# Forming gelu's argument inside a PSUM bank, and taking the order of all instructions from a table

## The chip, the cores and the metric

The kernel runs on one core of a Trainium2 chip. The metric is the device time of one execution, in microseconds (us). Before the change it is 719.35 us, the median of three runs (719.32 to 719.5).

The five engines are called here as the profile calls them: PE (TensorE, matrix products), ACT (ScalarE), DVE (VectorE), POOL (GpSimd), SP (SyncE, which issues most DMAs). Each engine works through its own list of instructions in the order in which the program put them there, and instructions of different engines are held apart by semaphores. PSUM, where PE writes its sums, is made of eight banks; one tile of 128x512 fp32 values fills one of them.

## The reference

A feed-forward layer on x of 4 sequences by 1024 tokens by 512 features, with a gate, and a residual:

```
scale = cond @ norm_w.T + 1.0
h = x * (scale * rsqrt(mean(x * x) + EPS))
val, gate = split(h @ up_w.T)               # 2 x 2048 columns
h = val * gelu(gate)
hq = act_quant(h)                           # 8-bit steps, by the largest |h| of a token
wq = weight_quant(down_w)                   # ternary
y = hq @ wq.T + x
```

## The kernel before, in words

**Tiling.** The four sequences are four batches of 1024 tokens. Each batch is cut in two halves of 512 tokens (TOK), and the 2048 gated columns in 16 groups of 128. One such group is a *slot*; 55 of the slots go through `slot()` (the first ones of the first batch go through simpler functions). A slot computes value and gate for both token halves, a 2x2 block product, by a scheme of seven products in place of eight. `product(c, g, ...)` is one of the seven (0 to 6): six matmuls of 128x512, since weights and activations are split in two fp16 parts, of which three cross terms over two halves of 256 features are kept.

**The slot's sums.** Three kinds of PSUM banks are used: two A, one B, two E. The products of slot g are laid into them so that sums which several results share are formed once:

- product 0 into bank A; ACT copies A to bank B; product 1 accumulates on B; ACT's gelu reads B into `t1` (the gate of the first half);
- product 4 into bank E; ACT copies E into `v` in SBUF;
- product 5 accumulates on A, which then holds 0+5. ACT copies this to `t2` in SBUF (L1217 to L1219, `first_value`);
- product 6 accumulates on A after that; DVE adds A into `v` (L1255);
- one slot later product 3 accumulates on A (0+5+6+3), and DVE multiplies it with `t1` into the result (L1239); product 2 accumulates on E (4+2), DVE adds E and `t2` into `t2` (L1249), ACT's gelu turns `t2` in place (L1252), and DVE multiplies it with `v` (L1258).

**The down projection.** The ternary weights of the down projection are fp8, and a second 2x2 scheme (class `Pair`, 11 pairs of token blocks) runs while the next batches' slots run, four pairs at a time in slots 10 to 13 of a batch, and three pairs at the end. A product of a pair is eight matmuls of 128x256 (L1413), which fill half of a PSUM bank. The pair's steps are spread over the slot: `first` forms product B11 in half 1 of bank k1, has ACT copy it to half 0 (L1421), and adds product B21 there; `third` accumulates product T2 on half 1 of k1 and has ACT copy that half to half 1 of bank k2 (L1430, 128x256); `fourth` goes on with B22 onto half 1 of k1, T3 on k2. Thus B21 and the copy touch different halves of the same bank k1. The last tokens go through a plain down projection (L1362).

**The order.** No function emits an instruction at once. The engines that the code calls are recorders: each call is kept as a step, and at the end a planner decides in which order the steps go out. In the kernel before this is class `Plan`: it works out which step needs which (by the regions that each reads and writes), gives each step a price, a due time and a place on its engine, runs some rounds of mending with chosen random seeds (`MENDS`), moves single steps by a list (`MOVES`), and `emit` then calls the real engines in the order of planned start times. The order within an engine, and where among PE's matmuls an ACT step is emitted, both come from there. The semaphores between engines are put in when the steps are emitted, from the order in which they are emitted.

**Start.** PE first runs warm-up matmuls (L1510), turns the first token tiles (L1494, L825) and then begins with the first slots (L1198, L1199); ACT loads its table for gelu in a step of its own (`start_t`, L1461) before it squares and scales x (L1480, L1487) and evicts the turned x (L1498).

## Time and profile before

| | |
|---|---|
| median of 3 runs | 719.35 us (719.32 to 719.5) |
| the profiled execution, its span | 717.4 us (the chain's last piece ends at 717.44) |
| what lies around the span (median less span) | 1.9 us |
| PE busy | 711.5 us (99%), 3625 matmul records |
| DVE busy | 605.2 us (84%) |
| ACT busy | 409.8 us (57%) |
| POOL busy | 130.0 us (18%) |
| granted TensorE clock | 1.000 |
| ACT copy `t<-A` (L1219) | 55 of 585 ns, 32.2 us |
| DVE add `t<-E,t` (L1249) | 55 of 689 ns, 37.9 us |

How to read it: the span is the time from the first to the last instruction that the profiler saw, and the time of a run is a little longer. A group of instructions is named by line, engine and operation, then out<-in with the shape. Idle time of an engine counts only where that engine, or one that waits for it, is on the path to the end. The busy time of PE includes matmuls that are in flight; one 128x512 matmul takes 379 ns from start to end, but the next starts long before.

### The profile page before, as it was taken

What the parts mean: (1) busy time and instruction counts of PE and PEld (TensorE: products, weight loads), DVE (VectorE), ACT (ScalarE), POOL (GpSimd) and SP (SyncE); (2) the same over time, 40 slices, a digit from 0 to 9 for tenths busy, and PEclk for the clock granted to TensorE, in tenths of its full rate; (3) what the DMA queues carried; (4) which work ended last, traced back from release to release, by engine and by line L of the source; (5) the groups of instructions that cost most, each with busy time, mean ns of one, the idle gap of its engine ahead of it and who ended that gap; (6) DMA issues with size and microseconds to landing.
All of it is one profiled execution on the core that took longest, in us unless ns stands there. A gap on an engine that the chain in (4) does not pass through costs nothing.

```text
span 717.4 us, 10113 instructions
## 1 busy us (share of the span) xinstructions
PE 711.5 (99%) x3625; PEld 355.8 (50%) x3625; DVE 605.2 (84%) x903; ACT 409.8 (57%) x671; POOL 130.0 (18%) x138
## 2 busy tenths in 40 slices
PE   8999999999999999999999999999999999999998
PEld 4544444444444456664444445665444444445744
DVE  7978998899899899878899887767878888956897
ACT  5677688784546897553435786533333775332454
POOL 4753141020100004660023003700011000000000
PEclk9999999999999999999999999999999999999999
DMA  7778999999785896759234555778233444453414
GB/s 261 253 205 208 240 227 252 194 257 268 219 227 133 210 245 173 223 153 211 67 101 110 118 129 142 176 191 173 73 118 103 102 102 99 99 98 104 150 57 146
DMA packets 189134, 118.74 MB, mean 166 GB/s; under 512 B 151302, under 2 KB 158359, under 8 KB 189084
## 3 DMA queue, kind: packets, MB, share of 16 engines
q1 hardware_dynamic: 188794, 117.77, 64.3%
q8 instruction: 28, 0.46, 0.3%
q10 hardware_dynamic: 290, 0.33, 0.1%
q14 instruction: 22, 0.18, 0.1%
HBM read 59.20 MB, written 23.09 MB: 115 GB/s over the span
## 4 chain that ended last, share of the span: by engine, by line
PE 97%; DMA 1%; ACT 1%; POOL 0%; DVE 0%; issue 0%; SPq 0%; POOLq 0%
PE A L1141 40%; PE E L1141 20%; PE B L1141 10%; PE po L1413 9%; PE E L1156 6%; PE A L1156 4%; PE B L1156 3%; PE po L1362 2%; PE E L1362 1%; PE A L1362 1%; DMA H<-in_x_dram 1%; PE B L1413 1%; PE B L1362 0%; PE A L1199 0%; PE po L1494 0%; PE po L825 0%
## 5 line engine op out<-in xcount | busy, mean ns | idle before, releaser
L1141 PEld LDWEIGHTS <-SXY 128*128 128x128 f16 x2184 | 213.7, 98 | 250.9
L1141 PE MATMUL A<-R,SXY 128*128 128x512 f16 x1188 | 276.3, 379 | 0.0
L1141 PE MATMUL E<-R,SXY 128*128 128x512 f16 x594 | 145.3, 379 | 0.0
L1334 DVE TENSOR_TENSOR H<-H,am 128x1024 f32<-128x1024 f32 x64 | 76.6, 1222 | 0.2
L1141 PE MATMUL B<-R,SXY 128*128 128x512 f16 x312 | 76.6, 379 | 0.0
L1275 DVE TENSOR_REDUCE gm<-H 128x512 f32<-128x1024 f32 x56 | 69.0, 1232 | 0.9
L1252 ACT ACTIVATE t<-t,sg 128x512 f32<-128x512 f32 x55 | 39.7, 721 | 51.0 <-DVE t L1249 51.0
L1239 DVE SCALAR_TENSOR_TENSOR H<-A,sg,t 128x512 f32<-128x512 f32 x55 | 41.2, 749 | 31.9 <-PE A L1141 31.6
L1291 POOL PARTITION_ALL_REDUCE am<-R x8 | 15.5, 1934 | 288.4 <-DVE R L1277 288.4
L1236 ACT ACTIVATE t<-B,sg 128x512 f32<-128x512 f32 x55 | 37.8, 687 | 42.7 <-PE B L1141 42.6
L1227 ACT COPY B<-A 128x512 f32<-128x512 f32 x55 | 31.4, 571 | 53.3 <-PE A L1141 53.1
L1249 DVE TENSOR_TENSOR t<-E,t 128x512 f32<-128x512 f32 x55 | 37.9, 689 | 28.2 <-PE E L1141 27.7
L1413 PE MATMUL po<-wd,R 128*128 128x256 fp8e4 (+1 forms) x448 | 57.0, 275 | 0.0
L1219 ACT COPY t<-A 128x512 f32<-128x512 f32 x55 | 32.2, 585 | 43.4 <-PE A L1141 39.0
L1255 DVE TENSOR_TENSOR v<-A,v 128x512 f32<-128x512 f32 x55 | 37.9, 690 | 20.4 <-PE A L1141 19.6
L1413 PEld LDWEIGHTS <-R 128*128 128x128 bf16 (+1 forms) x480 | 47.0, 98 | 13.1
L1231 ACT COPY v<-E 128x512 f32<-128x512 f32 x55 | 32.2, 586 | 31.9 <-PE E L1141 15.6
L1342 ACT ACTIVATE H<-H 128x1024 f32<-128x1024 f32 x38 | 39.7, 1049 | 8.5 <-DVE H L1334 8.3
L1258 DVE SCALAR_TENSOR_TENSOR H<-v,sg,t 128x512 f32<-128x512 f32 x55 | 41.7, 759 | 1.7 <-ACT t L1252 1.4
L1156 PEld LDWEIGHTS <-SXY 128*128 128x128 f16 x264 | 25.8, 98 | 30.5
L1346 ACT ACTIVATE R<-H 128x1024 bf16<-128x1024 f32 x38 | 39.6, 1052 | 1.0 <-DVE H L1086 0.5
L1277 DVE TENSOR_TENSOR R<-R,gm 128x512 f32<-128x512 f32 x56 | 38.4, 686 | 0.9
(270 smaller groups left out, 919.2 us busy)
## 6 DMA issues: line engine op xcount, KB each, us to landing
SXY<-s_dram SPq DMA_DIRECT2D x57, 256.0 KB, 2.7
H<-in_L_cond_up_w_dram SPq DMA_DIRECT2D x13, 512.0 KB, 4.1
SXY<-s_dram SPq DMA_DIRECT2D x15, 384.0 KB, 3.7
xr<-in_x_dram SPq DMA_DIRECT2D x19, 256.0 KB, 2.9
out_dram<-xr SPq DMA_DIRECT2D x19, 256.0 KB, 2.1
s_dram<-SXY SPq DMA_DIRECT2D x12, 384.0 KB, 3.6
s_dram<-SXY SPq DMA_DIRECT2D x5, 896.0 KB, 6.7
H<-in_x_dram SPq DMA_DIRECT2D x8, 512.0 KB, 4.8
```

Of the source, the lines that this page charges most:

```text
L1141: PE.matmul(o, s[:, w, k, :], xs(l, k), start=start and n == 0, stop=stop and n == len(TERMS) - 1, skip_group_check=True,)
L1156: PE.matmul(ps, a[k // 2][:, w, k % 2, :], XP[:, l, k, h * TOK : (h + 1) * TOK], start=n == 0, stop=n == len(terms) - 1,)
L1239: DVE.scalar_tensor_tensor(h_half(g - 1, 0), prev["A"], gain(g - 1, 0), prev["t1"], ALU.mult, ALU.mult)
L1249: DVE.tensor_tensor(prev["t2"], prev["E"], prev["t2"], ALU.add)
L1252: ACT.activation(prev["t2"], prev["t2"], AF.Gelu, scale=gain(g - 1, 1))
L1258: DVE.scalar_tensor_tensor(h_half(g - 1, 1), prev["v"], gain(g - 1, 0), prev["t2"], ALU.mult, ALU.mult)
L1275: DVE.tensor_reduce(gm[0], v, AX.X, ALU.max, apply_absolute_value=True)
L1277: return [largest, lambda: DVE.tensor_tensor(m, m, gm[0], ALU.max)]
L1334: DVE.tensor_tensor(v, v, r.to_broadcast([P, 2, TOK]), ALU.mult)
L1342: ACT.activation(v, v, AF.Copy, bias=MAGIC)
L1346: ACT.activation(q, by_tile(v), AF.Copy, bias=-MAGIC)
L1413: PE.matmul(po, w[:, j], m, start=start and j == 0, stop=stop and j == n - 1, skip_group_check=True,)
```

## The change

Two things are changed together.

**In the slot.** After product 5, ACT no longer copies bank A to `t2`. DVE adds A (which holds 0+5) and `v` (the kept product 4) into bank E, product 2 accumulates on E one slot later, and gelu reads E from PSUM into `t2`. The DVE add that stood behind product 2 is gone. So there are 55 ACT copies less, and 55 DVE adds stand at another place with other operands.

**In the order.** The planner is taken out: its dependency search, prices, due times, mending and moves. The steps are still recorded, and the order in which they are emitted is read from a table, `ORDER`, which holds the difference from each step's number to the next, packed as text.

```diff
         def first_value():
             product(5, g, cur["A"], False, True)
-            cur["t2"] = wpool.tile([P, TOK], F32, name=f"t2_{g}", tag="t2")
-            ACT.copy(cur["t2"], cur["A"])
+            DVE.tensor_tensor(cur["E"], cur["A"], cur["v"], ALU.add)
...
         if prev:
             product(2, g - 1, prev["E"], False, True)
-            DVE.tensor_tensor(prev["t2"], prev["E"], prev["t2"], ALU.add)
         mid[1]()
         if prev:
-            ACT.activation(prev["t2"], prev["t2"], AF.Gelu, scale=gain(g - 1, 1))
+            prev["t2"] = wpool.tile([P, TOK], F32, name=f"t2_{g}", tag="t2")
+            ACT.activation(prev["t2"], prev["E"], AF.Gelu, scale=gain(g - 1, 1))
...
-class Plan:
+class Book:
...
     def order(self):
 
-        steps = self.steps
...
-        for n in MENDS:
-            order, kept = self.mend(order, kept, random.Random(n))
-        return self.moved(order)
...
+        packed = zlib.decompress(base64.b85decode("".join(ORDER)))
+        order, at = [], 0
+        for n in range(0, len(packed), 2):
+            at += int.from_bytes(packed[n : n + 2], "little", signed=True)
+            order.append(self.steps[at])
+            at += 1
+        assert len({s.n for s in order}) == len(self.steps)
+        return order
+
+    def emit(self):
+        lines = {}
+        for s in self.order():
+            if s.line not in lines:
+                lines[s.line] = _at_line(s.line)
+            lines[s.line](s.do, s.args, s.kwargs)
+
+
+ORDER = (
+    'c-m!J37k%K_doX;qZzZA8M82!VF-~eYbaErO{<g^ylro9ucF@SEot#qDne1&Dy2;-3Pq@FWr>CeO=dC-hOv#oFwZ^z?>XmppJ(cS',
...
-    book.tied = False
...
-    book.emit(book.order())
+    book.emit()
```

Over the whole program PE has 3621 matmuls and 3558 weight loads, DVE 898 instructions, POOL 148 and SP 367 before and after; ACT has 54 fewer (55 copies less, one table load more). The order is another on every engine. Lines move up by some 360: what was L1141 (a product's matmul in later batches) is L782, L1413 is L1050, L1421 is L1058, L1430 is L1067, L1439 is L1076, L1498 is L1133, L1510 is L1145. The new DVE add is L859, the gelu that reads E is L892.

The places that the prediction speaks of follow. The first is PE at the beginning of the last three pairs (the third place in the program where pairs begin). `po_99` is bank k1 of the first of them, `xn_111` holds the operand of product T2, `R` here that of product B21. Before:

```order
L1413 LDWEIGHTS xn_111
L1413 MATMUL po_99<-wd,xn_111 128x256
L1413 LDWEIGHTS R
L1413 MATMUL B_90<-wd,R 128x512
L1413 LDWEIGHTS R
L1413 MATMUL B_90<-wd,R 128x256
```

This is the last of T2's eight matmuls on k1, and behind it a product of the next pair in bank `B_90`. In the change:

```order
L1050 LDWEIGHTS xn_111
L1050 MATMUL po_99<-wd,xn_111 128x256
L1050 LDWEIGHTS R
L1050 MATMUL po_99<-wd,R 128x256
L1050 LDWEIGHTS R
L1050 MATMUL po_99<-wd,R 128x256
L1050 LDWEIGHTS R
L1050 MATMUL po_99<-wd,R 128x256 [waits Activation_49]
```

Behind T2's last matmul stand here the eight matmuls of B21 on the other half of the same bank; the third of them waits for ACT, and what it waits for is the copy of half 1 (now L1067), which in turn waits for the second matmul of B21.

There are ten such copies from `po_99` to `po_97`. In the kernel before, between the matmul that releases the copy and the first later matmul on its bank, PE has at each of them at least six matmuls of 128x512, or eight of 128x256 and four of 128x512, on other banks. In the change five of the ten stand inside the eight matmuls of B21: at three (the first pair of batch 1's slots, the first pair of batch 2's, and the first of the last three pairs) nothing stands between, at one (second pair of batch 1) one matmul of 128x512, at one (fourth pair of batch 1) one of 128x256. At the other five there are at least six of 128x512, or nothing on PE waits for the copy soon.

The second place is ACT's list around the copy that belongs to it. Before:

```order
L1252 ACTIVATE t_1_123<-t_1_123,sg_124 128x512 [waits DVE_49]
L1421 COPY po_99<-po_99 128x256 [waits PE_49]
L1430 COPY po_97<-po_99 128x256 [waits PE_49,Activation_49]
L1421 COPY B_90<-B_90 128x256 [waits PE_49]
L1439 COPY po_97<-po_97 128x256 [waits PE_49,Activation_49]
```

In the change:

```order
L1058 COPY po_99<-po_99 128x256 [waits PE_49]
L892 ACTIVATE t_1_123<-E_100,sg_124 128x512 [waits PE_49]
L876 ACTIVATE t_0_105<-B_90,sg_124 128x512 [waits Activation_49]
L1067 COPY po_97<-po_99 128x256 [waits PE_49,Activation_49]
L1058 COPY B_90<-B_90 128x256 [waits PE_49,Activation_49]
```

The copy from `po_99` to `po_97` is the step of `third`. Its place among ACT's copies is nearly the same, but two gelus now stand between it and the copy of `first`.

The third place is ACT's list at the start of the program. `ssq` is the sum of squares of x, `rs` the factor of the norm, `start_t` a tile that nothing reads. Before:

```order
L1461 ACT_TABLE_LOAD
L1461 ACTIVATE start_t_85<-one 128x1 [waits DVE_49]
L1480 ACTIVATE H,ssq_0_87<-H 128x512 [waits DMAHW2_49]
L1480 ACTIVATE R,ssq_0_87<-H 128x512
L1480 ACTIVATE R,ssq_0_87<-H 128x512 [waits DMAHW3_49]
L1487 ACTIVATE H<-H,rs_0_88 128x512 [waits Activation_49,Pool_49]
L1487 ACTIVATE H<-H,rs_0_88 128x512 [waits DVE_49]
L1498 ACTIVATE R<-po_98,scT 128x512 [waits DVE_49,PE_49]
```

In the change:

```order
L1115 ACT_TABLE_LOAD
L1115 ACTIVATE H,ssq_0_87<-H 128x512 [waits DMAHW2_49]
L1115 ACTIVATE R,ssq_0_87<-H 128x512
L1115 ACTIVATE R,ssq_0_87<-H 128x512 [waits DMAHW3_49]
L336 DMA R<-in_cond_dram 128x384 [waits DMAHW0_49]
L1122 ACTIVATE H<-H,rs_0_88 128x512 [waits DVE_49,Pool_49]
L1122 ACTIVATE H<-H,rs_0_88 128x512 [waits Activation_49]
L1097 ACT_TABLE_LOAD
L1097 ACTIVATE start_t_85<-one 128x1
L1133 ACTIVATE R<-po_98,scT 128x512 [waits DVE_49,PE_49]
```

The step `start_t`, which needs the table that holds gelu, has moved behind the scaling of x, and with it a second table load stands right ahead of the first eviction (L1133).

More of the change, by code (lines that the diff above doesn't have):

```diff
@@ L96, with __init__ @@
 class Step:
-    __slots__ = (
-        "n", "eng", "do", "args", "kwargs", "line", "cost", "alone", "port", "before", "wait", "deps", "after", "late", "soon", "start", "end", "tied", "own",
-        "margin", "guard", "behind", "queue", "pre", "due",
-    )
+    __slots__ = ("n", "eng", "method", "do", "args", "kwargs", "line")
 class Engine:
-    def __init__(self, plan, name, real):
-        self._plan, self._name, self._real = plan, name, real
+    def __init__(self, book, name, real):
+        self._book, self._name, self._real = book, name, real
     def __getattr__(self, method):
```

452 lines of the change are left out of this document (85 added, 367 removed), and 14 rows, old and new, of tables (MENDS, MOVES).

## The prediction

> **What bounds the kernel now.** I read the page's busy shares and chain first, then the waits of PE, then the chain around one of the places that the change rearranges.
>
> ```profile
> PE 711.5 (99%) x3625; PEld 355.8 (50%) x3625; DVE 605.2 (84%) x903; ACT 409.8 (57%) x671; POOL 130.0 (18%) x138
> PE 97%; DMA 1%; ACT 1%; POOL 0%; DVE 0%; issue 0%; SPq 0%; POOLq 0%
> ...
> PE A L1510 <- DVE H L607: 1.3, 1, 1.3
> PE po L1494 <- DVE H L1489: 0.5, 1, 0.5
> PE B L731 <- DVE dg L725: 0.5, 1, 0.5
> PE B L1199 <- ACT R L1498: 0.4, 1, 0.4
> ...
> 25.00:714.33 689.33, 689.32 (x3519) 344.44 (x3517) 585.20 (x833) 395.36 (x641) 115.48 (x116) 1.00 0.64 162
> ```
>
> PE is the bound, at full clock, and almost without a gap: the list of its waits is complete with four rows, all before 15 us, and in the stretch from 25 us to its last matmul it is busy 689.32 of 689.33 us. So 32 us less of ACT copies is worth nothing by itself: ACT (57%) and DVE (84%) have no share in the chain there. PE does the same matmuls after the change. The time can fall only by what PE idles at the start, and rises by each gap that the new order makes in PE's list. A gain of DVE or ACT counts only where it closes such a gap; there are none after 25 us.
>
> The size of PE's steps comes from the chain at a pair's beginning:
>
> ```profile
> 271.96 1.51 PE A L1141 x7
> 273.47 0.87 PE po L1413 x8
> 274.34 1.29 PE E L1141 x6
> 275.63 1.42 PE po L1413 x13
> ```
>
> Six matmuls of 128x512 take 1.29 us, 0.216 each; eight of 128x256 take 0.87, 0.109 each. Fp16 and fp8 products alternate here at no extra cost, so the finer mixing of the new table costs nothing by itself.
>
> **The change, part by part.** *The slot.* These groups hold the work removed, moved and replaced:
>
> ```profile
> L1219 ACT COPY t<-A 128x512 f32<-128x512 f32 x55 | 32.2, 585 | 43.4 <-PE A L1141 39.0
> L1249 DVE TENSOR_TENSOR t<-E,t 128x512 f32<-128x512 f32 x55 | 37.9, 689 | 28.2 <-PE E L1141 27.7
> L1252 ACT ACTIVATE t<-t,sg 128x512 f32<-128x512 f32 x55 | 39.7, 721 | 51.0 <-DVE t L1249 51.0
> L1236 ACT ACTIVATE t<-B,sg 128x512 f32<-128x512 f32 x55 | 37.8, 687 | 42.7 <-PE B L1141 42.6
> L1255 DVE TENSOR_TENSOR v<-A,v 128x512 f32<-128x512 f32 x55 | 37.9, 690 | 20.4 <-PE A L1141 19.6
> L1275 DVE TENSOR_REDUCE gm<-H 128x512 f32<-128x1024 f32 x56 | 69.0, 1232 | 0.9
> ```
>
> ACT loses 55 copies of 585 ns (32.2 us). DVE's add keeps its count; its new form, PSUM plus SBUF into PSUM, is in no row, so I bound it by the add that also reads A and `v` (690 ns) and by that plus what the PSUM side might cost more, as between gelu from SBUF and from PSUM (721 against 687 ns, here even less): 0.66 to 0.73, and I take 690. Gelu reads PSUM as L1236 does, 687 in place of 721. All of this lies beside PE. What touches PE is when banks come free. Bank A is released for product 6 by an add of 690 instead of a copy of 585, 0.1 us later, and on an engine that is busy 84% instead of 57%. Bank E is released by gelu (687) where the add (689) did it: nothing. Behind product 2 the chain add, gelu, multiply loses its first link, 0.69 us earlier for L1258. Product 2 comes a slot after the new add, so that wait is covered by many matmuls. Cost of the slot on the path: 0, as long as product 6 finds some 0.8 us of other PE work behind product 5 (four matmuls of 128x512); if DVE is inside a reduction of 1.23 us when A is ready, this cover is gone and PE waits up to that long.
>
> *The order at the pairs.* This is where PE gets new waits. At five of the ten copies L1430 (L1067 in the change) the copy and the next matmul on the same bank now stand with nothing, one 128x512 or one 128x256 between. PE finishes a matmul of B21, ACT copies half 1, and only then may PE go on with B21 on half 0. The rows for the price:
>
> ```profile
> L1413 PE MATMUL po<-wd,R 128*128 128x256 fp8e4 x438 | 55.8, 273 | 0.0
> L1430 ACT COPY po<-po 128x256 f32<-128x256 f32 x10 | 3.6, 360 | 6.1 <-PE po L1413 6.1
> ...
> 23.76 0.37 ACT L852 CAST R<-po 128x256 f16<-128x256 f32 x1 [1.49 <-PE po L825]
> 24.18 0.14 PEld L825 LDWEIGHTS po<-ident,H 128*128 128x128 f32 x1 [0.22 <-ACT R L852]
> ...
> 713.50 0.82 PE L1362 MATMUL po<-wd,R 128*128 128x256 fp8e4 x6
> 714.36 0.48 DVE L1371 SCALAR_TENSOR_TENSOR R<-po,dq,R 128x256 f32<-128x256 f32 x1 [0.17 <-PE po L1362]
> ```
>
> The matmul lasts 273 ns to its end. From PE's end to the reader's start it takes 0.04 (714.32 to 714.36). The copy lasts 0.36. From ACT's end to PE it takes 0.05 (24.13 to 24.18). Without a wait PE would start the next matmul 0.109 after the last. The gap is 0.273 + 0.04 + 0.36 + 0.05 - 0.109 = 0.61 us. With a 128x512 between it is 0.61 - 0.216 = 0.40, with a 128x256 0.61 - 0.109 = 0.50. Sum: 3 x 0.61 + 0.40 + 0.50 = 2.73 us. The rows of 23.76 and 24.18 show that such a loop does stop PE already now: a cast of half a bank, 0.37 us, and the weight load that waited for it came 0.22 late. In the kernel before the same pair of steps (L1413, L1430) never stops PE, because 1.29 us of product matmuls on bank E stand behind T2 (the chain at 274.34), and the copy at 0.36 ends far inside them. Its cover is what the new order takes away. ACT may still be in an instruction when the copy is released, and the copy stands in line: with ACT busy 57% and instructions of 0.7 us this is 0.57 x 0.35 = 0.2 us on average for each place, 1.0 in all; below, nothing. Since two gelus with early operands stand ahead of the copy in the row shown, I take 0 and keep 1.0 for the range. Behind the stalled matmul everything on PE is late by the same amount, DVE and ACT with it, so nothing downstream absorbs it.
>
> The wait is between two halves of one bank, so it could look needless. The Trainium skill's page "PSUM — Partial Sum Buffer", section "PSUM bank collisions raise a hardware error", has the rule that speaks against this order: guard PSUM by bank and quadrant, not by address, since two engines at different addresses of one bank still collide. The rows of 24.18 agree, as PE went on to the bank only after the cast had ended; by the rule none of the five waits can go and the sum stays, and if halves counted apart it would be nothing.
>
> *The start.* The rows:
>
> ```profile
> 1.28 1.28 ACT L1461 ACT_TABLE_LOAD   x1 [1.28 <-PEq L2092]
> 2.58 0.20 ACT L1461 ACTIVATE start_t<-one 128x1 f32<-128x1 f32 x1
> ...
> 13.04 1.84 ACT L1498 ACTIVATE R<-po,scT 128x512 f16<-128x512 f32 x3 [1.57 <-PE po L1494]
> ...
> 11.52 0.20 PEld L1494 LDWEIGHTS po<-ident,H 128*128 128x128 f32 x2 [0.32 <-ACT H L1487]
> 11.91 0.42 PEld L825 LDWEIGHTS E<-ident,H 128*128 128x128 f32 x4 [0.19 <-POOL H L817]
> 14.36 1.60 PEld L1199 LDWEIGHTS <-SXY 128*128 128x128 f16 x8 [0.55 <-issue]
> 16.51 0.11 PEld L1199 LDWEIGHTS <-SXY 128*128 128x128 f16 x2 [0.55 <-ACT SXY L852]
> ...
> 3.37 2.31 PE L1510 MATMUL A<-H 128*128 128x512 f16 x5
> 22.80 0.69 POOL L817 TENSOR_SCALAR H<-H,iv 128x512 f32<-128x512 f32 x1
> ```
>
> The gaps before weight loads between 11 and 25 us add up to 0.32 + 0.19 + 0.55 + 0.55 + 0.22 = 1.83 us; that is the most that any order can win there, as the loads' ordinary spacing is in it. The new order puts two warm-up matmuls (L1510, 2.31 / 5, some 0.4 each and partly overlapping, so 0.4) among the turns and a POOL scaling of weights (0.69) ahead of the second x tile: up to 1.1 us lost. I take 0 and keep -1.83 and +1.1. The second table load, 1.28, and `start_t`, 0.20, are 1.48 us and fit into the 1.57 us in which ACT waits for the turned x: 0.
>
> The Trainium skill's page "ScalarE: Activation LUTs", section "What ACT_TABLE_LOAD costs", has a switch at about 1283 ns of load and 1380 ns of drain. The load of 1.28 agrees; the drain is not seen, for `start_t` began at 2.58, right behind the load, but nothing was in ACT then. By the rule the sum would be 1.3 us more.
>
> *The sum.* The profiled execution goes from 717.4 to 717.4 + 2.73 = 720.2 us of span. It lies 1.9 us under the median of runs, which stays around it: 719.35 + 2.73 = **722.1 us**.
>
> **The rivals.** (A) *The new add gates product 6.* Mechanism: DVE in a reduction of 1232 when A holds 0+5, so A comes free at 0.04 + up to 1.23 + 0.69 + 0.05 = 2.0 us, 0.7 past the cover of a product (1.29). For it: DVE at 84%. Against: DVE's reads of A (L1255, L1239) are of this kind now, and no PE gap comes of it. Two or three such slots among 55 give 1.6 us: 723.7. (B) *The second table load does not fit.* If ACT must empty before a load, 1.3 us more on the way to L1498 and so to L1199, as the chain runs through both: 723.4. For it: only 0.09 us is to spare in the gap. Against: ACT has waited for PE for a microsecond by then, so there is nothing left to empty.
>
> (C) *Not slower.* The copy is released by T2's own last matmul, not by the last one on its bank, so that the B21 matmuls that stand behind T2 cover it. Then at the last pairs two matmuls lie between, 0.61 - 2 x 0.109 = 0.39, at the fourth pair of batch 1 three, 0.28, at the other three more than 0.6 us: 0.67 in all, 720.0, which is no change. It decides once PE's signal for T2 is what ACT waits on. For it: the code needs no more than T2. Against: B21's matmul in the rows shown waits for ACT although ACT reads another half, so waits go by bank, and a copy that comes after two of B21 must then wait for them. (D) *Faster.* (C), or ACT so early that it costs nothing, and the start's gaps closed: 719.35 - 1.83 = 717.5. For it: ACT has 32 us more room and a new order at the start. Against: five waits stand in the list. (E) *The waits as forecast, and the start's whole gain*: 719.35 + 2.73 - 1.83 = 720.3, again no change.
>
> **How the numbers follow.** A measurement of this kernel cannot tell less than 0.2% (1.4 us) from no change, so "same" is 717.9 to 720.8. The forecast (722.1, with its bounds 721.0 to 723.1) gets 0.52, A 0.14, B 0.11, C 0.11, D 0.07, E 0.05. Slower is the forecast, A and B: 0.77; same C and E: 0.16; faster D: 0.07. The range leaves out D and half of A's upper tail: it begins at 719.9, under C, and goes to 724.2, where the forecast with both 1.0 of ACT's queue and 1.1 of the start would stand.
>
> **What would show it.** In the changed profile the list of PE's waits has rows of a matmul L1050 on `po` behind ACT's L1067, five in number, near 273, 289, 320, 445 and 665 us, each 0.3 to 0.6 us of idle time (a little less than the gaps above, since the matmul in flight counts as busy). If they are absent, C is right and the step on the pairs is wrong. If PE's waits name DVE L859 with `A`, A is right; if the start has ACT's L1133 later than 13.04 behind two table loads, B is. PE busy in the middle should stay within 0.1 us of its stretch but for these five; the copies of 585 ns should be gone from ACT with no effect on the end. The prediction is wrong if PE's last matmul ends before 716 us of the span.

## The result, and the profile after

| | before | changed | ratio (95% interval) |
|---|---|---|---|
| median | 719.42 us (719.32 to 719.63, 4 executions) | 723.23 us (722.36 to 724.32, 4 executions) | 1.0051 (1.0038 to 1.0064) |
| span of the profiled execution | 717.4 us | 721.6 us | |

The change makes the kernel slower by 0.5%: 3.8 us by the medians, 4.2 us by the two profiled spans. The forecast was 722.1 us, the range 719.9 to 724.2. Two executions that lie far off all the others are left out below: 812.54 us with a granted clock of 0.878 (the copy done twice), and 1534.94 us (the kernel before).

The busy shares of the changed kernel:

```profile
PE 712.2 (99%) x3625; PEld 356.4 (49%) x3625; DVE 594.0 (82%) x903; ACT 372.1 (52%) x617; POOL 126.8 (18%) x138
```

PE has the same 3625 matmul records and 0.7 us more of busy time. ACT has 37.7 us less work than before and DVE 11.2 us less, and the kernel is slower: neither engine was the bound.

The waits of PE in the changed kernel (what waited for what; microseconds in total, times, the longest). It is the whole list:

```profile
PE B L341 <- DVE one L248: 3.3, 1, 3.3
PE po L1050 <- ACT po L1067: 2.1, 5, 0.5
PE B L782 <- ACT B L867: 0.5, 1, 0.5
PE A L1145 <- DVE neghalf L246: 0.4, 1, 0.4
```

The second row is the forecast one: five waits of B21's matmuls (L1050) for the copy of `third` (L1067). The third row was not forecast. The first and the last are at the start, ahead of 10 us.

The timeline of PE, and then of ACT, around the five places (start, length, engine and line, and in brackets the idle time ahead and its releaser). The first place is at 273 us, the others follow:

```profile
273.45 0.38 PE L1050 MATMUL po<-wd,R 128*128 128x256 fp8e4 x2
274.33 0.49 PE L1050 MATMUL po<-wd,R 128*128 128x256 fp8e4 x3 [0.50 <-ACT po L1067]
...
290.37 0.82 PE L1050 MATMUL po<-wd,R 128*128 128x256 fp8e4 x6 [0.27 <-ACT po L1067]
...
320.93 0.60 PE L1050 MATMUL po<-wd,R 128*128 128x256 fp8e4 x4 [0.38 <-ACT po L1067]
...
446.00 0.27 PE L1050 MATMUL po<-wd,R 128*128 128x256 fp8e4 x1 [0.50 <-ACT po L1067]
...
666.75 0.93 PE L1050 MATMUL po<-wd,R 128*128 128x256 fp8e4 x7 [0.50 <-ACT po L1067]
```

```profile
273.93 0.36 ACT L1067 COPY po<-po 128x256 f32<-128x256 f32 x1 [0.46 <-PE po L1050]
```

At the first place two matmuls of B21 are through at 273.45 + 0.38 = 273.83. ACT starts the copy of the other half of the bank 0.1 later, at 273.93, and ends at 274.29. PE goes on at 274.33. A matmul in flight counts as busy, so the delay is the idle time plus the length of the last matmul less the spacing at which the next would have come: 0.50 + 0.273 - 0.109 = 0.66 us at the three bare places, 0.27 + 0.379 - 0.216 = 0.43 where a matmul of 128x512 lies between, and 0.38 + 0.273 - 0.109 = 0.54 where one of 128x256 does. Together 2.95 us.

The wait that was not forecast is at 213 us. PE, then ACT:

```profile
211.25 1.46 PE L782 MATMUL E<-R,SXY 128*128 128x512 f16 x6
213.18 1.46 PE L782 MATMUL B<-R,SXY 128*128 128x512 f16 x6 [0.47 <-ACT B L867]
```

```profile
208.84 1.06 ACT L602 ACTIVATE xr<-nx 128x1024 bf16<-128x1024 f32 x1 [3.29 <-DMA nx<-in_L_cond_down_w_dram]
...
210.47 1.04 ACT L602 ACTIVATE xr<-xt 128x1024 bf16<-128x1024 f32 x1
...
211.51 1.04 ACT L602 ACTIVATE xr<-xn 128x1024 bf16<-128x1024 f32 x1
...
212.55 0.58 ACT L867 COPY B<-A 128x512 f32<-128x512 f32 x1
```

ACT's copy of bank A to bank B, which product 1 needs, stands in ACT's list behind three preparations of the ternary weights (L602). The first of these waited 3.29 us for its DMA, so all three run just when the copy is wanted. The delay of PE is 0.47 + 0.379 - 0.216 = 0.63 us.

This wait belongs to the profiled execution and not to every one. In three kernels of the next section (the copies behind, the copies ahead, the copy done twice) ACT's list is the same here, but the first L602 starts at 207.69 to 208.12 us in place of 208.84, and PE has no such wait. With the copies behind, where that line is L609:

```profile
207.69 1.06 ACT L609 ACTIVATE xr<-nx 128x1024 bf16<-128x1024 f32 x1 [2.03 <-DMA nx<-in_L_cond_down_w_dram]
```

The last matmul of the changed kernel ends at 718.5 us, that of the kernel before at 714.33: 4.2 us later. The five waits are 2.95 of it and the wait at 213 us 0.63; the rest, some 0.6, arose ahead of 25 us. Behind that, the stretch from 25 us to the last matmul (length, then the busy times of PE, PE's weight loads, DVE, ACT and POOL) shows no other loss:

```profile
25.00:718.50 693.50, 690.87 (x3525) 344.89 (x3523) 574.59 (x833) 357.17 (x588) 114.65 (x118) 1.00 0.65 162
```

PE idles 693.50 - 690.87 = 2.63 us here. The five waits are 2.15 of idle time and the one at 213 us 0.47: 2.62 in all, which leaves nothing for anything else. The granted clock is 1.00.

The 0.6 us ahead of 25 us show in the first product of the first slots: in the kernel before, in the changed kernel, and in the kernel that has the slot alone (next section), whose start is in the order of the kernel before:

```profile
14.36 2.10 PE L1199 MATMUL B<-R,SXY 128*128 128x512 f16 x9 [0.37 <-ACT R L1498]
...
15.25 2.31 PE L840 MATMUL B<-R,SXY 128*128 128x512 f16 x9
...
14.85 2.10 PE L828 MATMUL B<-R,SXY 128*128 128x512 f16 x9 [0.37 <-ACT R L1121]
```

The changed kernel begins it 0.89 us late, and wins 0.3 of that back by 25 us. Two executions with the start of the kernel before differ by 0.49 at the same place, so it is not shown that all of the 0.6 comes from the order.

### The profile page after: what moved, and what is told of

It is laid out like the page before. It is cut to its first block, busy times and chain, and to the rows that moved or that the text cites. A ratio compares the mean times of both kernels' runs of the same rounds, so it can differ in the third digit from the quotient of the medians.

```text
span 721.6 us, 10034 instructions
## 1 busy us (share of the span) xinstructions
PE 712.2 (99%) x3625; PEld 356.4 (49%) x3625; DVE 594.0 (82%) x903; ACT 372.1 (52%) x617; POOL 126.8 (18%) x138
## 4 chain that ended last, share of the span: by engine, by line
PE 98%; ACT 0%; DVE 0%; issue 0%; ACTq 0%
PE A L782 39%; PE E L782 20%; PE B L782 10%; PE po L1050 9%; PE E L797 6%; PE A L797 4%; PE B L797 3%; PE po L1001 2%; PE E L1001 1%; PE A L1001 1%; PE A L1145 1%; PE B L1050 0%; PE B L1001 0%; PE B L840 0%; PE po L1129 0%; PE A L840 0%
## 5 line engine op out<-in xcount | busy, mean ns | idle before, releaser
L782 PEld LDWEIGHTS <-SXY 128*128 128x128 f16 x2184 | 213.7, 98 | 246.0 <-issue 1.4
L782 PE MATMUL A<-R,SXY 128*128 128x512 f16 x1188 | 289.6, 379 | 0.0
L782 PE MATMUL E<-R,SXY 128*128 128x512 f16 x594 | 154.7, 379 | 0.0
L782 PE MATMUL B<-R,SXY 128*128 128x512 f16 x312 | 80.2, 379 | 0.5 <-ACT B L867 0.5
L1050 PE MATMUL po<-wd,R 128*128 128x256 fp8e4 (+1 forms) x448 | 66.0, 275 | 2.1 <-ACT po L1067 2.1
L892 ACT ACTIVATE t<-E,sg 128x512 f32<-128x512 f32 x55 | 37.7, 687 | 46.2 <-PE E L782 46.2
L1050 PEld LDWEIGHTS <-R 128*128 128x128 bf16 (+1 forms) x480 | 46.9, 98 | 20.4 <-issue 2.5
L859 DVE TENSOR_TENSOR E<-A,v 128x512 f32<-128x512 f32 x55 | 38.2, 695 | 18.5 <-PE A L782 14.4
L797 PE MATMUL E<-R,SXY 128*128 128x512 f16 x132 | 30.0, 379 | 0.0
```

The costliest lines, as they stand in the source:

```text
L782: PE.matmul(o, s[:, w, k, :], xs(l, k), start=start and n == 0, stop=stop and n == len(TERMS) - 1, skip_group_check=True,)
L797: PE.matmul(ps, a[k // 2][:, w, k % 2, :], XP[:, l, k, h * TOK : (h + 1) * TOK], start=n == 0, stop=n == len(terms) - 1,)
L859: DVE.tensor_tensor(cur["E"], cur["A"], cur["v"], ALU.add)
L892: ACT.activation(prev["t2"], prev["E"], AF.Gelu, scale=gain(g - 1, 1))
L1050: PE.matmul(po, w[:, j], m, start=start and j == 0, stop=stop and j == n - 1, skip_group_check=True,)
```

## The experiments

In all of them the kernel before ran on the same chip beside the kernel of the experiment; its medians lie between 719.48 and 719.60 us. For a step that is moved, a list is added behind the reading of the table, of pairs (step, the step behind which it is now emitted). In the edits a line in brackets stands for the packed table.

### The copies moved behind B21

Each of the five copies of `third` comes behind the last or the next to last matmul of B21, so that most of B21 stands ahead of it. The sixth pair of numbers, at the last three pairs, holds the first matmul of T3, which writes the bank that the copy fills, behind the last of B22, so that it doesn't overtake the copy.

```diff
+        for n, after in MOVES:
+            order.remove(self.steps[n])
+            order.insert(order.index(self.steps[after]) + 1, self.steps[n])
         return order
+MOVES = (
+    (2225, 2166), (2367, 2313), (2654, 2600), (3537, 3483), (5134, 5115), (5170, 5169),
+)
```

> The changed kernel, with the five ACT copies that stood inside product B21 (third step of a pair) emitted later, behind the last or next to last matmul of B21, and one matmul of T3 that stood ahead of the last of them moved behind B22. Nothing else moves. Theory (five bank waits): the five waits of PE for the copy, 0.66 + 0.44 + 0.54 + 0.66 + 0.66 = 2.97 us between starts in the changed kernel's trace, are gone and nothing takes their place: 723.2 - 3.0 = 720.2 us, up or down 0.8 with the spread of the changed kernel's runs. Rival (a wait takes the place of another, since ACT and DVE stand late as well): 721.5 to 723, with new PE waits near the same places.

Measured: 720.92 us (720.37 to 721.54, 10 executions), ratio 1.0020 (1.0011 to 1.0029). The five waits are gone from the list; in their place stand two rows that the changed kernel did not have:

```profile
PE A L789 <- ACT B L874: 0.2, 1, 0.2
PE E L1008 <- DVE xr L1017: 0.2, 1, 0.2
```

So the five waits are a cause, and moving six steps gives back 2.3 us of the 3.8. It is less than the 2.95 that the trace put on them. With the five gone, PE runs ahead of the other engines: at the last tokens it now waits for DVE (0.18 + 0.34 us at 686 and 700 us), and at 285 us for a copy of A to B that stands behind a cast of 1.04 us on ACT (0.37 us). The two profiles agree on the sum: the last matmul ends at 715.90 us, 2.59 earlier than in the changed kernel. Of 2.95 for the five and 0.63 for the place at 213 us, where this execution has no wait, 0.89 goes to the new waits and 0.1 to a start that is later. The cast at 285 us:

```profile
283.53 1.04 ACT L733 CAST H<-xt 128x1024 f16<-128x1024 f32 x1 [0.80 <-POOL xt L709]
284.48 0.58 ACT L874 COPY B<-A 128x512 f32<-128x512 f32 x1
```

### The copies moved ahead of B21

Rival C said that the copy needs only T2's last matmul. Here four of the copies are emitted right behind it, ahead of B21 (at two places ahead of all but its first matmul, which stands ahead of T2), so that nothing of B21 can hold them.

```diff
+MOVES = (
+    (2367, 2366), (2654, 2653), (3537, 3536), (5134, 5133),
+)
```

> The changed kernel, with four of the five copies (all but the first) emitted earlier, right behind the last matmul of T2, whose half of the bank is the only one that the copy reads. So the copy is released by what it needs, and the matmul that then stands behind it on its bank is one of B21, on the other half. Theory (waits go by bank, whichever half is read or written): at three of the four places the wait only moves to an earlier matmul of B21 and stays 0.66, at the second it goes, for a product on another bank stands between: 0.66 (first place, untouched) + 0.66 x 3 = 2.6 us in four waits in place of 3.0 in five, 722.4 to 723.2 us. Rival (the wait came from a release that was late): the three waits fall by the two to four matmuls of 0.109 us that no longer stand ahead of the copy, 0.2 to 0.4 us or less each, 722 us or below.

Measured: 722.77 us (721.94 to 723.05, 5 executions), ratio 1.0042 (1.0028 to 1.0057).

```profile
PE po L1057 <- ACT po L1074: 2.0, 4, 0.5
```

The fifth copy, at 274 us, was not moved, and its wait is as it was. Of the four that were, three still stop PE, for as long as before (0.65 to 0.69 us of delay at 320, 444 and 666 us); at the fourth, near 288 us, seven matmuls of 128x512 on other banks stand between T2 and B21, and the wait is covered. That wait was 0.43, and the median is lower by 0.5; but the executions of the two kernels overlap, and in the profile the place at 213 us has no wait and the start is 0.3 later, so the gain is not shown to be this wait. PE and ACT at the last three pairs:

```profile
664.36 1.04 PE L1057 MATMUL po<-wd,xn 128*128 128x256 fp8e4 x8
...
665.90 0.82 PE L1057 MATMUL po<-wd,R 128*128 128x256 fp8e4 x6 [0.50 <-ACT po L1074]
```

```profile
665.49 0.36 ACT L1074 COPY po<-po 128x256 f32<-128x256 f32 x1 [0.96 <-PE po L1057]
```

The copy is released by T2's last matmul (664.36 + 1.04 = 665.40, 0.09 before the copy's start), as C had it. But now the first matmul of B21, which writes the *other* half of the bank, waits for the copy's end. Whichever is emitted first, the other engine waits: the dependency goes by the bank, or by the tile that fills it, which these runs can't tell apart. The prediction had cited the Trainium skill's page "PSUM — Partial Sum Buffer", section "PSUM bank collisions raise a hardware error", for this (guard by bank and quadrant, not by address); these rows agree in both directions. What shows is that the program's semaphores hold the two apart, not what would happen without them, which was not tried.

### The copy done twice

If the copy's length is a term of each wait, a second copy of the same half lengthens each wait by that much.

```diff
-        self.steps = []
+        self.steps, self.twice = [], set()
...
+            if s.n in self.twice:
+                lines[s.line](s.do, s.args, s.kwargs)
...
+            book.twice.add(len(book.steps))
```

> The changed kernel, with the ACT copy of a pair's third step done twice in a row at all eleven pairs (the second writes the same values). Theory (at five places PE waits for the copy itself): each of the five waits grows by one copy less the overlap of two ACT instructions, 0.36 - 0.1 = 0.26 us, and the six others stay hidden: 723.2 + 5 x 0.26 = 724.5 us, and the list of PE's waits for this copy goes from 2.1 to 3.4 us in five waits. Rival (the waits are a matter of release, not of the copy's length): 723.2 us, five waits of 2.1 us.

Measured: 725.04 us (724.91 to 725.75, 3 executions), ratio 1.0078 (1.0061 to 1.0095).

```profile
273.32 0.74 ACT L1070 COPY po<-po 128x256 f32<-128x256 f32 x2 [0.29 <-PE po L1052]
273.98 0.69 ACT L878 ACTIVATE t<-B,sg 128x512 f32<-128x512 f32 x1
...
274.12 0.49 PE L1052 MATMUL po<-wd,R 128*128 128x256 fp8e4 x3 [0.89 <-ACT po L1070]
```

Each of the five waits grows by 0.39 us, from 0.50 to 0.89 here, 1.95 in all, and a sixth place (679 us) loses 0.30. By the medians the kernel lost 1.8, by the spans 1.6, as the profiled execution has no wait at 213 us (0.63). So nothing of the copy's length is hidden at these places. The growth was expected at 0.26, with an overlap of 0.1 between the two copies. There is none: the second writes what the first has written, and the two take 0.74. The gelu behind them, which touches another bank, does begin 0.08 ahead of their end (273.98, and 273.32 + 0.74 = 274.06).

### The slot alone, in the old order

The prediction took the slot's own cost as 0, on a condition. Here the program of the changed kernel is emitted in the order of the kernel before; the new DVE add takes the place of the ACT copy that it replaces.

```diff
 ORDER = (
-    (the order of the change)
+    (the order of the kernel before, with the add L847 where the copy stood)
 )
```

> The changed slot (DVE adds A and v into E, gelu reads E, no ACT copy), emitted in the order of the kernel before: the new add stands where the ACT copy stood, and the few steps that would read or write a bank too early by that order wait for their turn. Theory (the order costs the time, the slot nothing but where the add gates a bank): the worked-out loops show two places at 155 and 165 us of PE work where the add is 0.31 and 0.09 us too slow, so 719.4 + 0.4 = 719.8 us, 719.4 to 720.5. Rival (the slot's edit costs a part of the 3.8 us by itself, since DVE frees bank A 0.1 us later and stands in line at 84%): 721 to 723.

Measured: 735.61 us (735.09 to 735.72, 4 executions), ratio 1.0220 (1.0205 to 1.0236). Both expectations were far too low. The waits of PE:

```profile
PE A L770 <- DVE E L847: 5.9, 11, 1.2
PE E L770 <- ACT t L880: 1.8, 2, 1.3
...
PE E L770 <- DVE E L847: 1.1, 1, 1.1
```

By the spacing of PE's matmuls the delays behind 25 us add up to 16 us, at 39 places of 0.1 to 1.4 us each. One of the smaller ones shows how they arise:

```profile
239.41 1.22 DVE L961 TENSOR_TENSOR H<-H,am 128x1024 f32<-128x1024 f32 x1
...
239.62 0.38 PE L770 MATMUL A<-R,SXY 128*128 128x512 f16 x1
239.84 1.46 PE L770 MATMUL E<-R,SXY 128*128 128x512 f16 x6
...
240.55 0.69 DVE L847 TENSOR_TENSOR E<-A,v 128x512 f32<-128x512 f32 x1
```

Bank A is complete at 239.62 + 0.38 = 240.00 us, while DVE is in an instruction of 1.22 us. The add begins at 240.55 and ends at 241.24, and product 6 starts at 241.29, where it would have started at 239.84 + 6 x 0.216 = 241.13. This is rival A's mechanism: one product of cover (1.29 us) is too little when DVE is inside a long instruction. The twelve waits for the add in the list are 7.0 us of idle time, and each delays PE by 0.16 more (a 128x512 in flight counts as busy for 0.379 and takes the place of 0.216), about 9 of the 16 us. With the places like the one shown, whose idle time is too short for the list, PE's waits for the add on bank A are 12.1 of the 16 us, at 34 places. At 32 of them DVE was inside an instruction when A was complete, at 16 in one of 1.2 us, at the others in shorter ones, often two in a row. The rest are waits on bank E: 2.3 us for gelu, 1.6 for the add. In the changed kernel's list there is no wait for the add at all. What else the new order does around it was not taken apart.

### The new order alone, with the old slot

The opposite crossing: the slot of the kernel before, in the order of the change. The ACT copy takes the place of the new add, and the old DVE add stands right ahead of its gelu.

```diff
-            DVE.tensor_tensor(cur["E"], cur["A"], cur["v"], ALU.add)
+            cur["t2"] = wpool.tile([P, TOK], F32, name=f"t2_{g}", tag="t2")
+            ACT.copy(cur["t2"], cur["A"])
...
+            DVE.tensor_tensor(prev["t2"], prev["E"], prev["t2"], ALU.add)
```

> The old slot (ACT copies A to t2, DVE adds E to t2, gelu on t2) in the new order: the ACT copy stands where the new add stood, the DVE add right ahead of gelu. Theory (the order costs the time): the five bank waits stay, 723.2 us as the changed kernel, 722.3 to 724.3; ACT has its 32 us of copies again, which may hold the five copies up a little more. Rival (the slot's edit is what costs): 719.4 to 721.

Measured: 740.63 us (739.92 to 741.59, 4 executions), ratio 1.0296 (1.0279 to 1.0313), again far above what was expected.

```profile
PE E L783 <- DVE t L891: 3.7, 6, 1.2
...
PE po L1052 <- ACT po L1069: 3.2, 5, 1.1
PE A L783 <- ACT t L861: 2.4, 2, 1.3
PE A L1052 <- ACT A L1069: 2.1, 1, 2.1
```

By the spacing of PE's matmuls the delays behind 25 us add up to 19.6 us. The five waits at the pairs are in this kernel too, two of them as long as in the changed kernel and three longer, 4.0 us in all; the eleventh copy of `third`, for which PE does not wait in the changed kernel, adds 2.3. The DVE add and the ACT copy that came back are 7.8, ACT's copies of A to B 3.2; the rest are other DVE steps. So this order has no room for the old slot's steps, and the change cannot be costed as the slot plus the order: each half alone costs 16 to 21 us, both together 3.8.

### The start alone

The old slot and the old order, but the first 350 steps in the order that the change gives them.

```diff
 ORDER = (
-    (the order of the change)
+    (steps 0 to 350 in the change's order, all others in that of the kernel before)
 )
```

> The slot and the order of the kernel before, but its first 350 steps (about the first 30 us) are emitted in the order that the table gives them among themselves; two table loads at the start come with it. Theory (the new start is part of the 3.8 us, because PE's warm-up begins at 3.3 in place of 1.3 us and the first x tiles are squared later on DVE): 0.5 us slower than before, 719.9 to 720.2 us, with the first B product of L1199 near 15.3 in place of 14.4 us. Rival (the start costs nothing, the rest of the 3.8 us is made of ACT's late copies in the middle): 719.3 to 719.6 us.

Measured: 719.77 us (719.33 to 720.16, 10 executions), ratio 1.0003 (0.9993 to 1.0012). The new start by itself costs 0.26 us by the medians, between the two expectations, which cannot be told from nothing.

Two kernels tried a mixture, which keeps the warm-up matmuls of the kernel before. In the first, steps 41 to 350 come in the change's order and all else, slot included, is as before:

```diff
 ORDER = (
-    (steps 0 to 350 in the change's order, all others in that of the kernel before)
+    (steps 41 to 350 in the change's order, all others in that of the kernel before)
 )
```

> The slot and the order of the kernel before, but steps 41 to 350 of its list are emitted in the order of the table, so that the first warm-up matmuls, DVE's constants and the first loads stand as before, and the turns and first products are mixed as in the change. Theory (of the new start only the late warm-up and the late square cost, and its mixing of turns and products closes gaps of PE that were 0.24 + 0.11 + 0.54 + 0.22 us before): 718.3 to 719.2 us, faster than the kernel before. Rival (x's landing sets when PE can begin, whatever the order): 719.4 us.

Measured: 719.98 us (718.94 to 724.37, 10 executions), ratio 1.0013 (0.9998 to 1.0027): no gain, and a wide spread: three executions (721.33, 721.4 and 724.37 us) have a mean granted clock of 0.995 to 0.997, the others 0.999 to 1.000. In the profiled execution, one of the others, PE idles 2.03 us ahead of the first turn of x:

```profile
11.29 0.33 PE L1118 MATMUL po<-ident,H 128*128 128x128 f32 x1 [2.03 <-DVE H L1113]
```

The second has the changed slot, the copies behind B21 (the first experiment's moves) and the first 40 steps in the order of the kernel before:

```diff
 ORDER = (
-    (the order of the change)
+    (steps 0 to 40 in the order of the kernel before, all others in the change's, with the first experiment's moves)
 )
```

> The changed kernel with the five copies behind B21 and the first 40 steps in the order of the kernel before. Theory (the two are separate): 720.9 less what the start gives back, 0.7 to 1.2 us: 719.7 to 720.2 us; what is then left against the kernel before are ACT's late copies of A to B in the middle, which differ from run to run. Rival (late copies grow when PE comes earlier, since ACT then waits in its list for DMAs and POOL just as long): 720.5 to 720.9 us.

Measured: 722.07 us (720.61 to 723.05, 5 executions), ratio 1.0032 (1.0018 to 1.0045): 1.2 us more than with the moves alone, where a gain was expected. Here too the executions fall in two groups: 722.07 to 723.05 us with a mean granted clock of 0.997 to 0.998 (three), and 720.61 and 720.86 with 1.000 and 0.999. The profiled execution is the one of 720.61, not slower than with the moves alone; PE idles 1.57 us in it ahead of the first turn, and 0.45 more is a copy on ACT at 212 us, the place that the next experiment is about. So the 1.2 us go with the three executions of lower clock, and what PE did in these was not recorded. In both profiled executions PE waits for DVE ahead of the turns; no gain of a start mended in pieces is shown.

### ACT's late steps moved behind the copy

This tests the wait at 213 us, which only some executions have. To the moves of the first experiment two are added: the L602 at 211.51 and the cast at 283.53 go behind the copy of A to B that had stood behind them.

```diff
 MOVES = (
     (2225, 2166), (2367, 2313), (2654, 2600), (3537, 3483), (5134, 5115), (5170, 5169),
+    (1592, 1737), (2118, 2323),
 )
```

> The changed kernel with the five copies behind B21, and two ACT steps emitted later, behind the copy of bank A to bank B that they stood ahead of: one sum of absolute down weights near 213 us, which follows others that wait for a DMA, and one cast of tokens near 284 us, which waits for POOL. Theory (ACT works its list in order, so a step that waits for something late holds up a copy that PE waits for): the waits of PE for this copy, 0.64 and 0.37 us in the traces so far, go and take most of the spread with them: 720.4 us, 720.0 to 720.8. What is left against the kernel before is then the start (0.3 us) and DVE at the end (0.5 us). Rival (some other step of ACT's list takes their place): 720.9 us, as without the two moves.

Measured: 720.43 us (720.26 to 720.79, 11 executions), ratio 1.0012 (1.0003 to 1.0021), as expected. No wait of PE for ACT is left. The executions now lie within 0.53 us of one another; those of the changed kernel lay within 1.96 (4 executions), those with the copies moved alone within 1.17 (10), and those of the kernel before on the same chip within 1.06 (20). This fits a time that follows the landing of the DMA where ACT's list holds a step that waits for one ahead of a step that PE needs; single executions were not compared with their landings. Against the kernel before 0.95 us are left by the medians. By the profiles the last matmul ends 1.19 later: 0.52 are two waits for DVE at the last tokens, and 0.67 arose at the start, where the wait ahead of the turns is 0.86:

```profile
PE po L1137 <- DVE H L1132: 0.9, 1, 0.9
...
PE E L1009 <- DVE xr L1018: 0.2, 1, 0.2
```

### Is there a version that beats both?

The old slot and order with steps 98 to 350 (the turns and the first slots) in the change's order, measured twice:

```diff
 ORDER = (
-    (steps 0 to 350 in the change's order, all others in that of the kernel before)
+    (steps 98 to 350 in the change's order, all others in that of the kernel before)
 )
```

> The slot and the order of the kernel before, but steps 98 to 350 of its list (from the second half of the first turns to about 30 us) are emitted in the order of the table. Warm-up, scaling of x and the first turns stand as before. Theory (PE's later gaps at the start, 0.54 and 0.22 us ahead of the first products, can be filled by mixing turns and products, and nothing makes PE idle longer ahead of the turns, so the clock stays whole): 718.8 to 719.2 us, faster than the kernel before by 0.3 to 0.7 us. Rival (the gaps only move, since ACT's evictions of the turned x set the pace): 719.4 to 719.6 us.

Measured: 718.96 us (718.68 to 719.99, 11 executions), ratio 0.9994 (0.9985 to 1.0003).

> The kernel with the old slot, the old order and the table's order in steps 98 to 350, once more beside the one above. Theory: 718.9 to 719.1 us, 0.4 to 0.6 us below the kernel before, and 0.6 us below the fully mended change. Rival (the gain of the first look was chance): 719.3 to 719.6 us.

Measured: 719.18 us (718.89 to 720.53, 11 executions), ratio 0.9996 (0.9987 to 1.0005). Both medians lie 0.4 to 0.5 us under the kernel before, and both intervals hold 1: 0.06% is less than these runs can tell.

The last kernel joins this start to the changed slot with all eight moves:

```diff
 ORDER = (
-    (the order of the change)
+    (steps 0 to 350 as in the kernel just shown, all others in the change's order with the eight moves)
 )
```

> The changed slot, in the table's order with the five copies behind B21 and the two ACT steps behind the copy of A to B, and with the first 350 steps as in the kernel with the old turns. So every wait of PE that the changed kernel had beyond those of the kernel before is undone but DVE's at the end. Theory (the causes add up): 720.4 less 0.3 (new start) less 0.5 (mixed products behind the old turns) = 719.6 us. Rival (PE, being earlier by that, meets DVE earlier at the end, and the waits there, 0.18 and 0.34 us, grow by what is won): 720.2 to 720.4 us.

Measured: 720.49 us (720.12 to 721.71, 11 executions), ratio 1.0015 (1.0006 to 1.0024). Neither expectation holds, though the rival's number is nearly met: the waits at the last tokens did not grow (0.18 and 0.34), and what the start gained is lost at 42 us, where the two lists meet. PE's row, and ACT's two instructions ahead of it:

```profile
PE A L797 <- ACT t L821: 0.7, 1, 0.7
```

```profile
40.61 1.04 ACT L493 CAST H<-H 128x1024 f16<-128x1024 f32 x1 [4.45 <-POOL H L470]
41.57 1.26 ACT L821 ACTIVATE t<-A,sg 128x512 f32<-128x512 f32 x2
```

It is the pattern of 213 us again: a cast that had waited 4.45 us for POOL stands ahead of a gelu that PE needs. No version here is shown to beat the kernel before.

## Why the prediction was right, and where it was not

**What bounds the kernel.** Right. ACT lost 37.7 us of work and the kernel lost 3.8 us of time; the loss can be read from PE's gaps alone.

**The order at the pairs.** Right in mechanism, in the five places (274, 290, 321, 446 and 667 us; forecast 273, 289, 320, 445 and 665) and in direction, and shown by moving the copies away (the waits are gone) and by doubling them (each grows by the copy's length). The mis-sized term is the hand-over from PE to ACT: 0.04 us in the sum and 0.09 measured (273.83 to 273.93 in the rounded rows). With it the loop is 0.273 + 0.09 + 0.36 + 0.05 - 0.109 = 0.66 us against 0.61, and the five are 2.95 against 2.73. The 0.04 was taken from a hand-over of PE to DVE, but it is no matter of the engine. In the kernel before, this very copy starts 0.04 after PE's end (288.59 + 1.04 = 289.63):

```profile
288.59 1.04 PE L1413 MATMUL po<-wd,R 128*128 128x256 fp8e4 x8
...
289.66 0.36 ACT L1430 COPY po<-po 128x256 f32<-128x256 f32 x1 [0.24 <-PE po L1413]
```

It does so at seven of its eleven places there (at one ACT is still busy), and starts 0.09 after at the three of the last pairs. There the copy waits for two semaphores, as the list in the section on the change shows, and the wait for PE stands in an instruction of its own ahead of it. In the changed kernel it stands so at all five places. The queue of ACT, taken as 0 at these five places, was 0.

**The sum.** Forecast +2.73, measured +3.81 by the medians and +4.2 by the profiled spans. In the profiled execution the miss of 1.4 is 0.2 of the hand-over, 0.6 of the start, and 0.63 of a term that the sum did not have: a copy on ACT at 213 us behind steps whose DMA was late. The prediction had looked for ACT's queue at the ten copies of the pairs, but ACT's list has another order everywhere, and the place that mattered was elsewhere. How often that wait comes in other executions is not known. That the time lies inside the range is in part luck: the range had its upper room from ACT's queue at the pairs (1.0, and it was 0) and from the start (1.1), not from this wait.

**The start.** Taken as 0 between -1.83 and +1.1. In the changed kernel some 0.6 us, alone in the old order 0.26 (not told from 0): the first product is 0.89 late, and 0.3 is won between it and 25 us. A gain against the kernel before is not shown.

**The second table load.** Taken as 0, right. ACT's timeline at the start of the changed kernel:

```profile
10.88 1.33 ACT L1122 ACTIVATE H<-H,rs 128x512 f32<-128x512 f32 x2 [1.85 <-POOL rs L650]
12.23 1.28 ACT L1097 ACT_TABLE_LOAD   x1
13.53 0.20 ACT L1097 ACTIVATE start_t<-one 128x1 f32<-128x1 f32 x1
13.75 0.69 ACT L1133 ACTIVATE R<-po,scT 128x512 f16<-128x512 f32 x1
```

The load begins 0.02 us after the end of the scaling before it (10.88 + 1.33 = 12.21) and `start_t` 0.02 after the load. The prediction weighed the Trainium skill's page "ScalarE: Activation LUTs", section "What ACT_TABLE_LOAD costs", which adds a drain of 1380 ns to a load of 1283. The load agrees; no drain is seen, this time with an instruction in ACT right ahead. The sign that the prediction named for B did come, L1133 later than 13.04 behind two table loads, but it could not tell B from a late turn. By the program this eviction waits for the sixth of PE's turns on the `po` banks:

```profile
13.44 0.38 PE L1129 MATMUL po<-ident,H 128*128 128x128 f32 x2
```

The first of these two ends at 13.44 + 0.27 = 13.71, so the eviction at 13.75 could hardly have begun earlier without the load. So rival B did not occur.

**The slot.** The cost of 0 is right for this kernel, but the reasoning was too easy. It took as evidence that DVE's other reads of A cause no gap now; the slot alone in the old order shows that whether such a read costs anything is a property of the order around it. In the old order rival A's mechanism, an add that comes late because DVE is inside another instruction, makes most of the 12.1 us on bank A. Its price, 0.7 us a place, lies inside the 0.1 to 1.4 measured there; its count, two or three among 55, is far under the 34. The new add takes 695 ns where 690 was taken (660 to 730 as the bounds), and gelu from PSUM 687, as taken:

```profile
L859 DVE TENSOR_TENSOR E<-A,v 128x512 f32<-128x512 f32 x55 | 38.2, 695 | 18.5 <-PE A L782 14.4
L892 ACT ACTIVATE t<-E,sg 128x512 f32<-128x512 f32 x55 | 37.7, 687 | 46.2 <-PE E L782 46.2
```

**The rivals that ended lower.** C fell: its release by T2's matmul was produced on purpose, and B21 waited all the same. D and E needed a start without gaps, which the changed order does not make.

**Nothing downstream absorbs it.** Not quite. When the waits of 2.95 us were taken away, PE met DVE at the last tokens (0.52 us) and ACT at 285 us (0.37), where before the waits had given these engines time: 0.89 of the 2.95 would have been lost there without them.

What stays open: how the 0.6 us ahead of 25 us in the changed kernel divide among the single steps of the start and the landing of x, in how many executions the wait at 213 us comes, and what the executions with a lower clock have in common.

## What to carry to other kernels

When an order of instructions changes, look on the busiest engine for the places where two instructions on the same PSUM bank, with another engine's access between them, have moved together: in these runs each such loop cost the last matmul's length, the hand-over, the other engine's access and the hand-over back, less one spacing, whichever halves of the bank they touched. Then go through the lists of the other engines for steps that wait for a DMA or a slow engine and stand ahead of a step that the busiest engine needs: that is where lost time came from here, and it seems a spread between executions too. Do not cost a changed operation and a changed order apart if the order was made for the operation.

## What was not expected of the hardware

The hand-over from PE to a reader has two lengths, for ACT and for DVE alike. In the kernel before, 103 of the 192 that end a wait of ACT (of more than 0.1 us) take 0.04 to 0.05 us and 89 take 0.08 to 0.10; of DVE's 132, 92 take 0.04 to 0.05 and 40 take 0.09 to 0.11. Each of the longer ones has a semaphore instruction right ahead of the reader, and none without one is longer than 0.05: where a reader waits for two semaphores, one wait stands in an instruction of its own, and the way over it is 0.05 longer. PE's ends are modelled in the profile, so the difference is safer than the lengths. From ACT's end back to PE it is 0.05.

In the kernel with PE idle for 2.03 us ahead of the turns in its profiled execution, the mean granted clock of single executions fell to 0.995 and 0.997 (724.37, 721.33 and 721.4 us) and was 0.999 to 1.000 in the others (718.94 to 720.36 us). The kernel with the moves and the older start shows the same two groups (1.57 us of idle time in its profile). The Trainium skill's page "TensorE: Matmul & The Clock Gate", section "What's actually happening", lets the clock fall after an idle window of about 3.4 us. The profiled executions show 2.03 and 1.57 us; how long PE idled in the slower executions was not recorded, so whether the rule holds here stays open.
